# Sixteen tables of a graph layer, made four tiles earlier from the second group on

## The chip, the cores and the metric

One core of a Trainium2 chip. The metric is the device time in microseconds of one execution; lower is better. A profiled execution of the same kernel gives the durations below.

## The reference

Eight graphs share one adjacency matrix of 2048 nodes, with about nine neighbours for a node. Two attention layers follow each other, each with a residual and a layer norm. Layer 0 is scaled dot-product attention whose softmax runs apart in chunks of 256 nodes; layer 1 is a graph attention layer with leaky ReLU logits.

```python
# layer 0: x is (8, 2048, 256), 4 heads of 64, 8 chunks of 256 nodes
scores = clip(einsum('bhnd,bhjcd->bhnjc', q, kc) / 8, -10, 10)
scores = where(mask == 0, -10, scores)
attn = softmax(scores, axis=-1)                     # over each chunk
ctx = einsum('bhnjc,bhjcd->bhnd', attn, vc)
out = layernorm(ctx @ Wo.T + bo + x) * gamma + beta
x = layernorm(x + out)
# layer 1
e = leaky_relu(s_src[:, :, None, :] + s_dst[:, None, :, :], 0.2)
alpha = softmax(where(adj != 0, e, -inf), axis=2)
x = layernorm(x + elu(einsum('bijh,bjhd->bihd', alpha, Wh)))
```

## The kernel before

The adjacency is sparse, so the kernel builds lists of neighbours and gathers rows, in place of dense products. `edge_lists` runs first. It reads the 16 row tiles of the matrix, takes the largest 24 column numbers of each row on DVE, and ranks the nodes by their number of neighbours; each node's record is then scattered to HBM at its rank (L118, 16 indirect DMAs of POOL) and read back sorted (`srt`, L122). From `srt` come `node`, `idx`, `valid` and `same`. Sorted in this way, tile t of 128 nodes needs `CAPS[t]` neighbours, 24 for the first and 5 for the last.

The eight graphs are worked in four groups of two (`g` is 0 to 3), each with 16 tiles. For a group, **tables** have to stand in HBM: `tables(g, t)` makes keys and values (`kv_d[g]`, 512 KB a tile) and queries (`qx_d[g]`) of 128 rows. It loads `x` for two tiles at a time (L320), transposes it on PE (L336), copies it on ACT (L338, L341), multiplies on PE (L372, L376, L385, with biases by L313), copies to `kvs` (L367, L378, L379) and `qs` (L389) on ACT and stores both from SP's queue (L380, L391). `kvs` and `qs` have one buffer each, the PSUM tag `tk` has two. For every second tile POOL adds beta to `x` (L351) and SP stores the sum (L352). A table of group 1 holds a column more, the rank.

The tables of group 0 are made while the lists are: `edge_lists` calls `between(it)` after each of its 16 row tiles. The tables of group g+1 are made in the main loop, one with each tile of group g.

A tile of layer 0 goes through `fetch0` (POOL gathers one row of `kv_d` per neighbour, L489, and the queries, L527), `scores0` (products on DVE, L547 and L554, summed on PE, L566 and L576), `softmax0`, `context0` (weights on DVE, L501, or ACT, L507; sums on PE, L514; copy to `cT`, L626), and a tile later `finish0` and `rows1`, which writes the tables of layer 1. Gathered rows go into a ring of 14 units of two rows: 5 live in `ring0`, 9 in `ring1`, which takes the room that `edge_lists` has left and is zeroed first (L442 on ACT, L444 on DVE).

The main loop follows `seq`: 32 tiles of layer 0 (groups 0 and 1), then layer 0 of groups 2 and 3 with one tile of layer 1 between each two, then the rest of layer 1. `fetch(k + 1)` gathers for the next step ahead of this step's work. A gather may read any row of its table, so it waits for all 16 tiles of `kv_d[g]`. At the last tile of a group, `tables_first` holds the fetch back until the last table has been made. Instructions of one engine keep the order that a scheduler gives them, which follows the order of the program where the data allow no better.

The lines that carry this in the loop:

```python
tables_first = layer == 0 and seq[k + 1][0] == 0 and seq[k + 1][1] % NT == 0
if not tables_first:
    fetch(k + 1)
...
if g + 1 < NG:
    tables(g + 1, i % NT)
if tables_first:
    fetch(k + 1)
```

Of the kernel before, what the change touches and what calls it, by code (L numbers as in the profile page):

```python
# [9 lines left out]
F32 = mybir.dt.float32  # L10
# [7 lines left out]
P = 128  # L18
# [24 lines left out]

def edge_lists(tc: tile.TileContext, pool, bank, adj, const, ident, rec_d, B, between):

# [3 lines left out]
    NT = N // P  # L53
# [43 lines left out]
        between(it)  # L97


    rank = const.tile([P, NT], F32, name="rank")  # L100
    rank_i = pool.tile([P, NT], I32, name="rank_i")

    half = NT // 2
# [4 lines left out]
    for it in range(half):  # L108
        gt = pool.tile([P, N], F32, tag="v", name="v", bufs=2)
        nc.vector.tensor_scalar(gt, krow, key[:, it:it + 1], 0.0, op0=ALU.is_gt, op1=ALU.add,  # L110
                                accum_out=rank[:, it:it + 1])
        junk = pool.tile([P, N], BF16, tag="junk", name="junk", bufs=1)
        k = half + it
        nc.scalar.activation(junk, krow, AF.Sign, bias=nkey[:, k:k + 1], accum_out=rank[:, k:k + 1])
        nc.vector.tensor_scalar(rank[:, k:k + 1], rank[:, k:k + 1], 0.5, 0.5 * (N - 1), op0=ALU.mult, op1=ALU.add)
        nc.vector.tensor_copy(rank_i.rearrange("p (h t) -> p t h", h=2)[:, it], rank.rearrange("p (h t) -> p t h", h=2)[:, it])
        for k in (it, half + it):
            nc.gpsimd.indirect_dma_start(out=views[k],  # L118
                                         out_offset=bass.IndirectOffsetOnAxis(ap=rank_i[:, k:k + 1], axis=0),
                                         in_=rec[:, k, :], in_offset=None)  # L120
    srt = pool.tile([P, NT, REC], F32, name="srt")
    nc.sync.dma_start(srt, rec_d.rearrange("(t p) r -> p t r", p=P))  # L122

    vals = srt[:, :, 0:TOP]
    node = const.tile([P, NT], I32, name="node")
    nc.vector.tensor_copy(node, srt[:, :, TOP + 2])
    valid = const.tile([P, NT, TOP], I8, name="valid")
# [4 lines left out]
    idx = const.tile([P, NT, TOP], I32, name="idx")  # L132
    nc.vector.tensor_copy(idx, far)
    nodeb = const.tile([P, NT, 2 * G], I32, name="nodeb")
# [10 lines left out]
    same = []  # L145
# [21 lines left out]
    nc.tensor.matmul(op, nbad, ones, start=True, stop=True)  # L167
    over = const.tile([1, 1], I32, name="over")
    nc.vector.tensor_copy(over, op)
    return idx, valid, same, node, nodeb, rank, over  # L170


@with_exitstack
def sparse_path(ctx: ExitStack, tc: tile.TileContext, keep, x, adj, Wq, bq, Wk, bk, Wv, bv, Wo, bo, gamma, beta, W, a,
                out):
    nc = tc.nc
    B, N, F = x.shape
    KC = F // P
    NT = N // P
    NCH = N // CH  # L180
    NG = B // G
# [4 lines left out]
    rec_d = nc.dram_tensor("rec_d", [N, REC], F32).ap()  # L186
# [12 lines left out]
    const = ctx.enter_context(tc.tile_pool(name="const", bufs=1))  # L199
    ident = const.tile([P, P], F32, name="ident")  # L200
# [216 lines left out]
        tables(0, t)  # L417


    rings, turn = [ctx.enter_context(tc.tile_pool(name="ring0", bufs=1))], [0]  # L420

    def unit():
# [8 lines left out]

    with tc.tile_pool(name="lists", bufs=1) as pool:
        with nc.allow_low_precision("exact small integers"):
            idx, valid, same, node, nodeb, rank, over = edge_lists(tc, pool, bank, adj, const, ident, rec_d, B,
                                                             first_tables)
        nc.vector.tensor_copy(keep, over)

    rings.append(ctx.enter_context(tc.tile_pool(name="ring1", bufs=1)))
# [85 lines left out]
    def fetch0(g, t):  # L524
        units = gather(kv_d[g].shape[1], kv_d[g], idx, t)
        qx = work.tile([P, 2 * GF], F32, tag="qx", name="qx", bufs=4)
        nc.gpsimd.indirect_dma_start(out=qx, out_offset=None, in_=qx_d[g],  # L527
                                     in_offset=bass.IndirectOffsetOnAxis(ap=node[:, t:t + 1], axis=0))
        got0[g, t] = qx, units
# [80 lines left out]
    def context0(g, t):  # L610
        S = CAPS[t]
        al = st0.pop((g, t))
        units = got0[g, t][1]
        acc = bank("acc").rearrange("p (c r) -> p c r", r=P)

        na = len(units) // 4
        if g == PG:
            places(t, units)
        for u, s0, n in units[len(units) - na:]:
            weighted_act(u[:, :, GF:2 * GF], al, s0, n)  # L620
        for i, (u, s0, n) in enumerate(units):
            if i < len(units) - na:
                weighted(u[:, :, GF:2 * GF], al, s0, n)
            summed(acc, u[:, :, GF:2 * GF], s0 == 0, s0 + n == S)
        cT = work.tile([P, G * KC, P], F32, tag="cT", name="cT", bufs=1)
        nc.scalar.copy(cT, acc)  # L626
        st0[g, t] = cT
# [44 lines left out]
    def fetch1(p, t):  # L672
        got1[p, t] = gather(2 * WW, wh_d[p], idx1, t)

    def softmax1(p, t):
        S = CAPS[t]
        units = got1[p, t]
        z = small.tile([P, 2, GH, S], F32, tag="z1", name="z1")
        for u, s0, n in units:
            nc.vector.tensor_tensor(z[:, :, :, s0:s0 + n].rearrange("p k e s -> p s k e"),  # L680
                                    u.rearrange("p s (k w) -> p s k w", k=2)[:, :, :, GF:GF + GH],
                                    sd[p % 2][:, t].unsqueeze(1).to_broadcast([P, n, 2, GH]), op=ALU.add)
        z = z.rearrange("p k e s -> p (k e) s")
        nc.vector.scalar_tensor_tensor(z, z, SLOPE, z, op0=ALU.mult, op1=ALU.max)

        neg = small.tile([P, S], F32, tag="neg", name="neg")
        nc.vector.tensor_scalar(neg, valid[:, t, 0:S], -1.0, 1e30, op0=ALU.add, op1=ALU.mult)
        nc.vector.tensor_tensor(z, z, neg.unsqueeze(1).to_broadcast([P, 2 * GH, S]), op=ALU.add)
        m = small.tile([P, 2 * GH], F32, tag="m", name="m")
        nc.vector.tensor_reduce(m, z, axis=AX.X, op=ALU.max)  # L690
        nc.vector.tensor_tensor(z, z, m.unsqueeze(2).to_broadcast([P, 2 * GH, S]), op=ALU.subtract)
        e = z
        nc.scalar.activation(e, z, AF.Exp)
        nc.vector.tensor_tensor(e, e, valid[:, t, 0:S].unsqueeze(1).to_broadcast([P, 2 * GH, S]), op=ALU.mult)
        r = small.tile([P, 2 * GH], F32, tag="r", name="r")
        nc.vector.tensor_reduce(r, e, axis=AX.X, op=ALU.add)

        nc.vector.tensor_scalar(r, r, 1e-30, None, op0=ALU.max)
        nc.vector.reciprocal(r, r)
        nc.vector.tensor_tensor(e, e, r.unsqueeze(2).to_broadcast([P, 2 * GH, S]), op=ALU.mult)  # L700
        st1[p, t] = e
# [62 lines left out]
    seq = [(0, i) for i in range(2 * NT)]  # L764
# [24 lines left out]
    def scatters():  # L789
        for f in late:  # L790
            f()
        late.clear()

    def at(i):
        return i // NT, order[i % NT]

    def at1(i):
        return i // NT, order[i % NT] if i >= NT else order1[i]
# [3 lines left out]
    def fetch(k):  # L802

        while fetched[0] <= min(k, len(seq) - 1):
            layer, i = seq[fetched[0]]
            (fetch1(*at1(i)) if layer else fetch0(*at(i)))
            fetched[0] += 1
# [3 lines left out]
    for k, (layer, i) in enumerate(seq):  # L811
        g, t = at1(i) if layer else at(i)
        between = layer == 0 and seq[k + 1][0] == 1
        tables_first = layer == 0 and seq[k + 1][0] == 0 and seq[k + 1][1] % NT == 0
        if not tables_first:
            fetch(k + 1)
        scatters()
        if layer == 0:
            scores0(g, t)
            if between and i + 1 < NG * NT:  # L820
                softmax1(*at1(seq[k + 1][1]))
            if waiting is not None:

                if waiting:
                    finish1(*at1(waiting - 1))
                context1(*at1(waiting))
                waiting = None
            if i > 1:
                rows1(*at(i - 2))
            if i:  # L830
                finish0(*at(i - 1))
            if g + 1 < NG:
                tables(g + 1, i % NT)
            if tables_first:
                fetch(k + 1)
            softmax0(g, t)
            context0(g, t)
        elif seq[k - 1][0] == 0 and seq[k - 1][1] + 1 < NG * NT:
            waiting = i
        else:  # L840

            last = seq[k - 1] == (0, NG * NT - 1)
            if last:
                rows1(*at(NG * NT - 2))
                finish0(*at(NG * NT - 1))
            softmax1(g, t)
            if last:
                rows1(*at(NG * NT - 1))
            finish1(*at1(i - 1))
            context1(g, t)  # L850
            if i >= NT + 2:
                release(g - 1, i - NT - 2)
# [434 lines left out]
```

## Time and profile before

| what | us |
|---|---|
| median of 3 runs | 2400.64 |
| the three runs | 2385.87 to 2404.24 |
| profiled execution | 2397.55 |
| its span, first to last instruction | 2395.8 |
| `srt` issued, first gather of group 0 | 188.3, 195.2 |
| first `cT`, last `cT` of group 0 | 246.8, 617.5 |
| last `cT` of group 1, of group 2, of group 3 | 1002.1, 1448.1, 1951.6 |

The page of the profile gives busy time by engine over the span, a timeline in 40 slices, and groups of instructions by line. From the same trace come answers for a window: the busy time of each engine in it (the number of instructions in brackets), who waited for whom, and the instructions of an engine in order of time, each with its start, its duration and, in square brackets, the idle time ahead of it and what ended it. A busy PE counts matmuls with modelled ends, so it is not PE at its peak. `POOL` indirect DMAs are counted by the time of making their descriptors.

Two groups of the page around the tables:

```profile
L351 POOL TENSOR_TENSOR xt<-xt,beta_r 128x1024 f32<-128x1024 f32 x32 | 77.1, 2410 | 143.1 <-PE tk L336 126.3
L385 PE MATMUL tk<-wq,xT 128*128 128x256 f32 x512 | 145.2, 397 | 24.4 <-ACT kvs L379 24.4
```

Behind the shape stand the number of instructions, their busy time and mean duration in ns, the idle time ahead of them, and what ended most of it.

### The profile page before, as it was taken

The page shows a single profiled execution, that of the slowest core. Times are in us where ns is not written, and L with a number is a line of the kernel's source. Part 1 is how long each engine was busy: PE and PEld are TensorE (multiplying, and loading weights), DVE is VectorE, ACT ScalarE, POOL GpSimd, SP SyncE. Part 2 cuts the span into 40 slices and gives each one's busy share as a digit, 9 for nine tenths or more (in the row PEclk, how much of TensorE's full clock was granted, in tenths as well). Part 3 has the DMA queues.
Part 4 walks back from the last instruction along what each step waited for, and adds up shares of the span by engine and source line. Part 5 has one row for each costly group of instructions (what it writes and reads, how often), then busy time and mean ns, then how long its engine had stood idle before and what let it go on. Part 6 is the DMA issues. An engine that isn't in the chain of part 4 may idle for free. (4 is left out here: it accounts for less than half of the span.)

```text
span 2395.8 us, 38844 instructions
## 1 busy us (share of the span) xinstructions
PE 1900.4 (79%) x11946; PEld 1622.0 (68%) x11946; DVE 1833.5 (77%) x4099; ACT 1409.0 (59%) x5036; POOL 1505.0 (63%) x1230
## 2 busy tenths in 40 slices
PE   7686889889899898999988885888678786664764
PEld 5565677778778787777876774776566675554653
DVE  6864587877588988588988886887788887775775
ACT  4573455546566555655565665664356677665766
POOL 3125455672666676376668856774677685787883
PEclk9897899899999999999998997987878987877887
DMA  7737877795889798598879977896679896786884
GB/s 259 242 137 272 265 270 281 260 346 209 316 287 320 260 334 319 212 388 298 302 258 353 360 281 238 285 321 221 230 274 326 306 319 248 278 310 231 302 296 154
DMA packets 239982, 669.10 MB, mean 279 GB/s; under 512 B 43688, under 2 KB 70059, under 8 KB 237719
## 3 DMA queue, kind: packets, MB, share of 16 engines
q0 software_dynamic: 156800, 505.01, 60.1%
q1 hardware_dynamic: 79248, 151.55, 17.2%
q10 hardware_dynamic: 3718, 9.97, 1.3%
q8 instruction: 98, 1.61, 0.3%
q14 instruction: 118, 0.96, 0.1%
HBM read 612.79 MB, written 126.36 MB: 309 GB/s over the span
## 5 line engine op out<-in xcount | busy, mean ns | idle before, releaser
L489 POOL DMA_INDIRECT u<-kv_d,idx x656 | 810.2, 1235 | 436.4 <-PE acc L514 185.7
L514 PE MATMUL acc<-ident,u 128*128 128x128 f32 x5248 | 713.4, 291 | 157.0 <-DVE u L501 89.0
L514 PEld LDWEIGHTS acc<-ident,u 128*128 128x128 f32 x5248 | 637.5, 151 | 220.7 <-DVE u L501 133.2
L489 POOL DMA_INDIRECT u<-wh_d,idx x328 | 416.5, 1270 | 148.2 <-issue 76.4
L566 PE MATMUL pr<-ident,u 128*128 128x128 f32 (+1 forms) x1984 | 287.0, 295 | 78.7 <-DVE u L547 77.2
L501 DVE TENSOR_TENSOR u<-u,al 128x1024 f32<-128x1024 f32 x280 | 334.5, 1234 | 1.5
L566 PEld LDWEIGHTS pr<-ident,u 128*128 128x128 f32 (+1 forms) x1984 | 245.4, 151 | 110.8 <-DVE u L547 104.6
L547 DVE TENSOR_TENSOR u<-u,qx 128x1024 f32<-128x1024 f32 (+1 forms) x248 | 302.0, 1218 | 18.3 <-DMA u<-kv_d,idx 15.1
L501 DVE TENSOR_TENSOR u<-u,z 128x1024 f32<-128x1024 f32 x266 | 314.4, 1212 | 0.6
L507 ACT ACTIVATE u<-u,z 128x64 f32<-128x64 f32 x1008 | 262.0, 337 | 25.0 <-DVE z L700 17.1
L507 ACT ACTIVATE u<-u,al 128x64 f32<-128x64 f32 x800 | 209.1, 342 | 23.2 <-DVE al L607 22.3
L663 PE MATMUL mf<-wa,x1T 128*128 128x264 f32 x512 | 167.6, 455 | 23.1 <-ACT x1T L658 14.8
L351 POOL TENSOR_TENSOR xt<-xt,beta_r 128x1024 f32<-128x1024 f32 x32 | 77.1, 2410 | 143.1 <-PE tk L336 126.3
L385 PE MATMUL tk<-wq,xT 128*128 128x256 f32 x512 | 145.2, 397 | 24.4 <-ACT kvs L379 24.4
L451 ACT ACTIVATE nm<-sums 128x2 f32<-128x2 f32 (+1 forms) x160 | 32.4, 202 | 221.3 <-DVE sums L641 122.6
L372 PE MATMUL tk<-wkv,xT 128*128 128x256 f32 x512 | 151.7, 410 | 12.9 <-ACT xC L341 12.6
L635 PE MATMUL mf<-wo,cT 128*128 128x256 f32 x512 | 148.4, 415 | 6.3 <-ACT whs L666 5.3
L376 PE MATMUL tk<-wkv,xC 128*128 128x256 f32 x512 | 144.5, 399 | 0.0
L663 PEld LDWEIGHTS mf<-wa,x1T 128*128 128x128 f32 x512 | 101.7, 218 | 59.7 <-ACT x1T L658 23.6
L455 ACT ACTIVATE sq<-o,nm 128x256 bf16<-128x256 f32 x256 | 129.7, 507 | 5.3
L554 DVE TENSOR_TENSOR u<-u,qx 128x1024 f32<-128x1024 f32 (+1 forms) x96 | 116.0, 1214 | 16.6 <-DMA qx<-qx_d,node 7.1
L590 DVE TENSOR_SCALAR sc<-tf 128x64 f32<-128x64 f32 (+5 forms) x64 | 14.0, 218 | 138.2 <-PE tf L576 138.2
(168 smaller groups left out, 3254.0 us busy)
## 6 DMA issues: line engine op xcount, KB each, us to landing
kv_d<-kvs SPq DMA_DIRECT2D x48, 512.0 KB, 6.0
wh_d<-whs SPq DMA_DIRECT2D x64, 260.0 KB, 5.8
xt<-in_x_dram SPq DMA_DIRECT2D x64, 256.0 KB, 4.8
qx_d<-xt SPq DMA_DIRECT2D x32, 512.0 KB, 4.4
qx_d<-qs SPq DMA_DIRECT2D x64, 256.0 KB, 5.8
x_d<-o SPq DMA_DIRECT2D x64, 256.0 KB, 5.2
xr<-x_d SPq DMA_DIRECT2D x32, 512.0 KB, 4.9
u<-kv_d,idx POOLq DMA_INDIRECT x656, 6.5
```

Of the source, the lines that this page charges most:

```text
L372: nc.tensor.matmul(pm[:, 0:F], xT[:, b * KC + kc, rows], wkv[:, kc, 0:F], start=(kc == 0), stop=False, skip_group_check=True)
L376: nc.tensor.matmul(pm[:, F:], xC[:, b * KC + kc, rows], wkv[:, kc, F:], start=False, stop=(kc == KC - 1), skip_group_check=True)
L385: nc.tensor.matmul(qb, xT[:, b * KC + kc, rows], wq[:, kc, :], start=(b == 0 and kc == 0), stop=False, skip_group_check=True)
L455: nc.scalar.activation(sq, src[:, k, :], AF.Square, bias=nm[:, k:k + 1], accum_out=m2[:, k:k + 1])
L489: nc.gpsimd.indirect_dma_start(out=u[:, k, 0:width], out_offset=None, in_=table, in_offset=bass.IndirectOffsetOnAxis(ap=idx[:, t, s0 + k:s ...
L501: nc.vector.tensor_tensor(pv, pv, av, op=ALU.mult)
L507: nc.scalar.activation(pe, pe, AF.Copy, scale=al[:, e, s0 + k:s0 + k + 1])
L514: nc.tensor.matmul(acc[:, c, :], part[:, k, c * P:(c + 1) * P], ident, is_transpose=True, start=first and k == 0 and c == 0, stop=last and ...
L547: nc.vector.tensor_tensor(prod.rearrange("p k j (s w) -> p k j s w", w=W8), u[:, :, 0:GF].rearrange("p s (k j w) -> p k j s w", k=UNIT, w=W8),
L566: nc.tensor.matmul(pr[0:n * W8, k, :], prod[:, j // (NJ // UNIT), j % (NJ // UNIT), :], ident, is_transpose=True, start=(j == 0), stop=(j ...
L635: nc.tensor.matmul(po[:, b, :], cT[:, b * KC + kc, :], wo[:, kc, :], start=(b == 0 and kc == 0), stop=False, skip_group_check=True)
L663: nc.tensor.matmul(pw[:, 0:F + 2 * H], xT[:, b * KC + kc, :], wa[:, kc, :], start=(kc == 0), stop=(kc == KC - 1))
```

## The change

`edge_lists` gets one more function to call, `behind`. It is called after the 16 scatters and ahead of the load of `srt`; it makes the tables (1,0) to (1,3). In the main loop, the tile with number i then makes the table that lies 4 further on than before: tables(g+1, t) with t from 4 to 15, and after them the first four of group g+2. Tiles 44 to 47 make none. The fetch of the next step stands ahead of the step's work in every case. `rank`, which the tables of group 1 read, is now allocated ahead of `edge_lists` and passed in.

```diff
-def edge_lists(tc, pool, bank, adj, const, ident, rec_d, B, between):
+def edge_lists(tc, pool, bank, adj, const, ident, rec_d, rank, B, between, behind):
...
-    rank = const.tile([P, NT], F32, name="rank")
     rank_i = pool.tile([P, NT], I32, name="rank_i")
...
                                          in_=rec[:, k, :], in_offset=None)
+    behind()
     srt = pool.tile([P, NT, REC], F32, name="srt")
     nc.sync.dma_start(srt, rec_d.rearrange("(t p) r -> p t r", p=P))
...
+    LEAD = 4
+
+    def lead_tables():
+        for t in range(LEAD):
+            tables(1, t)
+
+    rank = const.tile([P, NT], F32, name="rank")
...
-        tables_first = layer == 0 and seq[k + 1][0] == 0 and seq[k + 1][1] % NT == 0
-        if not tables_first:
-            fetch(k + 1)
+        fetch(k + 1)
...
-            if g + 1 < NG:
-                tables(g + 1, i % NT)
-            if tables_first:
-                fetch(k + 1)
+            if i + NT + LEAD < NG * NT:
+                tables(*divmod(i + NT + LEAD, NT))
             softmax0(g, t)
```

More of the change, by code (lines that the diff above doesn't have):

```diff
@@ L42, with edge_lists @@
 EMIN = 4.5399929762484854e-05
-def edge_lists(tc: tile.TileContext, pool, bank, adj, const, ident, rec_d, B, between):
+def edge_lists(tc: tile.TileContext, pool, bank, adj, const, ident, rec_d, rank, B, between, behind):
     nc = tc.nc
@@ L169, in edge_lists @@
     nc.vector.tensor_copy(over, op)
-    return idx, valid, same, node, nodeb, rank, over
+    return idx, valid, same, node, nodeb, over
 @with_exitstack
@@ L433, in sparse_path @@
         with nc.allow_low_precision("exact small integers"):
-            idx, valid, same, node, nodeb, rank, over = edge_lists(tc, pool, bank, adj, const, ident, rec_d, B,
-                                                             first_tables)
+            idx, valid, same, node, nodeb, over = edge_lists(tc, pool, bank, adj, const, ident, rec_d, rank, B,
+                                                             first_tables, lead_tables)
         nc.vector.tensor_copy(keep, over)
```

## The prediction, made before the result was known

> **What bounds the kernel now.** I read the totals of the page first, then the busy time in stretches cut at the milestones of the tiles, then the waits of the opening, and last the timelines of ACT and POOL at the two places that the change touches.
>
> ```profile
> PE 1900.4 (79%) x11946; PEld 1622.0 (68%) x11946; DVE 1833.5 (77%) x4099; ACT 1409.0 (59%) x5036; POOL 1505.0 (63%) x1230
> ```
>
> No engine is full over the whole span, so the stages have to be read apart. The columns below are PE, weight load, DVE, ACT and POOL busy, the granted clock, the share of the DMA engines and GB/s.
>
> ```profile
> 176.00:187.00 11.00, 0.21 (x1) 0.00 (x0) 0.00 (x0) 0.58 (x3) 8.23 (x8) 0.73 0.51 177
> 187.00:200.00 13.00, 11.61 (x47) 9.17 (x48) 3.34 (x16) 5.15 (x21) 3.86 (x4) 0.63 0.50 134
> ...
> 210.00:222.00 12.00, 4.16 (x13) 3.19 (x14) 9.64 (x8) 10.67 (x11) 6.30 (x6) 0.72 0.76 259
> ...
> 357.00:617.00 260.00, 232.59 (x1491) 200.10 (x1490) 199.04 (x375) 139.70 (x520) 145.58 (x115) 0.93 0.76 264
> 617.00:1002.00 385.00, 349.80 (x2249) 300.19 (x2248) 306.15 (x617) 227.61 (x896) 241.94 (x190) 0.96 0.83 296
> ...
> 1300.00:1399.00 99.00, 85.65 (x581) 74.73 (x582) 80.85 (x166) 63.52 (x234) 79.54 (x60) 0.93 0.95 352
> ...
> 1460.00:1490.00 30.00, 13.62 (x63) 11.42 (x64) 18.02 (x53) 16.78 (x60) 14.75 (x14) 0.61 0.60 206
> ```
>
> From 357 to 1002 us (groups 0 and 1) PE is busy 232.6 + 349.8 of 645 us, 90%: PE bounds there, and work that is moved from one of these tiles to another gains nothing. The opening has room: from 176 to 300 us PE is busy 89.3 of 124 us. The hole at 1460 to 1490 us comes just after the third group boundary.
>
> The waits of the opening (194 to 300 us: who waited for whom, total, times, longest):
>
> ```profile
> DVE sc L590 <- PE tf L576: 26.6, 4, 11.2
> ACT kvs L367 <- DMA kv_d<-kvs: 22.8, 4, 8.6
> POOL u L489 <- PE acc L514: 17.5, 3, 16.9
> PEld tf L576 <- ACT prT L572: 13.4, 4, 6.2
> ```
>
> These are one chain. ACT may refill kvs, which has one buffer, only when its table has landed; behind that wait on ACT stands the copy prT (L572), for it waits PE, for PE waits DVE. The boundary into group 3, on POOL's timeline:
>
> ```profile
> 1401.81 2.37 POOL L351 TENSOR_TENSOR xt<-xt,beta_r 128x1024 f32<-128x1024 f32 x1
> 1416.46 1.87 POOL L489 DMA_INDIRECT u<-wh_d,idx  x1 [12.27 <-ACT sq L455]
> ...
> 1432.85 1.00 POOL L489 DMA_INDIRECT u<-kv_d,idx  x1 [7.82 <-issue]
> ```
>
> POOL gathers almost nothing from 1400 to 1433 us, because the first tile of group 3 needs the whole of kv_d3, whose last piece is issued at 1425.7 us. The longest PE wait of 1399 to 1500 us, 14.0 us for the weighted u of L501, is the hole above. The same gap of POOL stands at the first boundary (557.0 to 610.1 us) and the second (940.3 to 994.0), but there PE goes on at 90%.
>
> **What the Trainium skill says.** "TensorE: Matmul & The Clock Gate", in its table ahead of the first section, gives ScalarE and GpSimd a strict first-in first-out queue: so one wait for kvs holds everything behind it. The trace agrees: the exp of the first tile comes after three such waits. The same page, "What's actually happening", says that idle time brings the clock down: here 0.61 in the hole at 1460 us against 0.96 in group 1. "SBUF — State Buffer", "The DMA setup-cost knee", fits a transfer as 2 us plus bytes over 436 GB/s: for a 512 KB table an estimate of 3.2 us. The trace has 6.2 us as median, under other traffic, and 7.5 to 8.6 us from issue to ACT's next copy in the opening. I use the trace.
>
> **The change, part by part.** I also read the order of the instructions of both compiled programs, engine by engine.
>
> *Price of a table, from its lines at full clock.* PE, from 154.7 to 160.7 us, takes 6.1 us for one, and 0.6 us of transposes: 6.7 us. ACT: 4 copies of 0.37, one of 0.59, 0.19 for the rank column, and half a pair of chunk_x, 2 x (0.39 + 0.2 + 0.49) = 2.2: 4.4 us. POOL: half of a 2.4 us beta addition. SP: two stores, half of two loads and of a store. DVE: none, apart from one small sum in the last tile of a group. Nothing is added or removed in all: 64 tables stay 64, and SP, ACT and POOL issue the same DMAs in another order.
>
> *Opening.* The old program already makes tables (1,0) and (1,1) here: their pieces go out at 203.9 and 221.8 us. So the change moves two more ahead of the first context, and the rest of the four by the sixth tile: counted on ACT at the first cT, 19 tables before and 21 after, at tile 5 22 and 26. Of PE, 4 x 6.7 = 27 us are put into a stretch with 34.7 us idle (124 - 89.3), but ACT's queue decides: ahead of the first exp stand 5 waits of L367 for kvs in place of 3, and ahead of the first cT 6 in place of 4. Followed along ACT: L367 of (1,1) at 211.3 as before; (1,2) at 221, as one turn of kvs takes 7.5 us to land and some 2 us of copies and issue; now the zeroing of ring1 on ACT (L442, 5 x 1.93 us), which started at 212, starts here, so POOL's gathers into ring1, that waited for it until 214.2, go on at 223; (1,3) at 234; (1,4) at 244, and then the exp, at 232.3 before: +12. The first cT comes at about 254.5, before at 246.8: +8. Two tables are still to be caught up until tile 5, 13 us of PE, of which the 12% idle of these 100 us may take most. POOL also has one beta addition (2.4 us) ahead of the first gather and one between the gathers of tiles 0 and 1, each waiting for PE; they end before L442 does. SP: the read of the flag and the stores of group 1 change places; the flag is read at the end only. I take **+11 us**; bounds +3 (PE catches up in idle time) and +27 (all four in series).
>
> *First two boundaries.* The fetch of the next tile now stands ahead, its table complete four tiles earlier. What the gap costs: tiles 20 to 27 of group 1 (105 records) took 212.9 us from cT to cT, tiles 28 to 31 (30 records) 84.1; so a tile costs 13.6 us and a record 0.99. Tiles 15 to 19 (35 records) ought to take 102.7 and took 105.9; tiles 31 to 35 took 102.9. The gap costs 3.2 + 0.2: **-3 us**; the 14 ring units cover the rest. Bounds 0 and -12 (PE's dip of about 5 us at 610 to 660 and 3 us at 1010, with the slow clock).
>
> *Third boundary.* Here layer 1 runs beside, and behind tile 48 stand 24 gathers of one layer-1 tile at 1.3 us each. Pairs of tiles in group 3 (no tables) took 6.3 us + 1.81 per record, fitted to tiles 51 to 62; pairs (47,48) and (49,50) with 22 and 39 records took 53.2 and 80.2, 7 and 3 over it: **-10 us**. Bounds -3 and -25, nearly the 30 us for which POOL stood.
>
> *Four tables fewer beside tiles 39 to 47* (ACT's counts: 8.5 before, 5 after). PE is 87% busy at 1300 to 1399, DVE 82%, POOL 80%: not one bound. By the fit, pairs (43,44) and (45,46) took 6.4 us too long each with some 1.5 tables, pairs (39,40) and (41,42) took 9 and 5 less than it. I take 2.3 us for each of 3.5 tables: **-8 us**; bounds 0 and -24 (3.5 x 6.7).
>
> Sum: 11 - 3 - 10 - 8 = **-10 us**. The profiled execution took 2397.55 us (span 2395.8 and 1.75 around it), which gives 2387.6; it lies 3.1 us under the median of the three runs, 2400.64, which gives 2390.6. I say 2389.
>
> **Rivals.** *Faster by over 1%*: the opening takes the tables in idle time (+3), and the boundaries and the emptier third stretch give most of their bounds (-8, -20, -18): -43, 2357 from the median. For it speak the 34.7 us of idle PE and the 33 us without gathers; against it PE's 90% and the covered first boundaries. *Slower*: ACT's queue with the single kvs buffer becomes the bound of the opening. If each of the four tables costs its whole turn of 9.5 us there, the tiles start 38 us late, and as PE bounds until 1002 us nothing is caught up; with 8 us of gain later this is +30, 2430. It is over 1% from a cost of 24 us above the later gains on. For it speaks the 22.8 us already spent in this wait and two more waits ahead of the first tiles; against it that PE, not ACT, is full from tile 5 on. *It does little*: the order found by the scheduler already filled the gap, so opening and ends cancel: 2398 to 2403.
>
> **How the numbers follow.** About 1% (24 us) is what a measurement of this kernel can tell from no change, as its three runs lie 18 us apart. Forecast with small gain 0.40 and little change 0.17: within 1% 0.57. Faster case 0.25, slower case 0.18. The range from 2352 to 2430 reaches the centres of both; the likeliest case alone spans 2375 to 2405.
>
> **What would show it.** The first exp at about 244 and first cT near 254 us; kv_d1 complete near 520 us and no gap of POOL above 15 us at the three boundaries; the hole after 1460 us gone; from the fourth group on the same distances from cT to cT as now. It would be wrong if the first tiles come over 25 us late, if tiles 5 to 15 still fall back, or if the hole only moves to another layer-1 tile.

## The result, and the profile after

The changed kernel takes 2404.07 us (median of 20 runs, 2391.76 to 2415.28). The kernel before, now with 20 runs of its own, takes 2386.57 (2377.1 to 2404.24), 14 us under the median of its first three. The ratio is 1.0073, 95% interval 1.0053 to 1.0092: a loss of 17.5 us, where a gain of 10 was summed. On some chips a part of the runs takes longer, so ratios compare only the runs within 1.5% of the fastest of the same kernel.

Lines up to some 340 of the changed kernel are the old number plus 1, those of the loop plus 11. First the totals of the page, then the waits of the opening (194 to 310 us; total, times, longest):

```profile
PE 1893.1 (79%) x11946; PEld 1629.1 (68%) x11946; DVE 1833.6 (76%) x4099; ACT 1410.2 (59%) x5036; POOL 1500.4 (62%) x1230
```

```profile
POOL u L500 <- PE acc L525: 25.5, 4, 9.7
ACT kvs L368 <- DMA kv_d<-kvs: 23.5, 7, 7.0
```

The busy times are those of before within 0.5%, so the loss lies in waits. ACT's wait for `kvs` comes 7 times, not 4, and takes as long. The milestones say where time went; all are starts of copies to `cT`, one profiled execution for each column. after_again and a_pl2 are two runs told of below:

| stretch, by tiles | before | after | after_again | a_pl2 (copies pinned) |
|---|---|---|---|---|
| first `cT` | 246.8 | 253.5 | 254.9 | 252.8 |
| to the end of group 0 (tile 15) | 617.5 | 617.4 | 616.9 | 617.0 |
| group 1 (15 to 31) | 384.6 | 395.9 | 393.3 | 381.4 |
| of it first boundary, 15 to 17 | 51.4 | 41.0 | 42.7 | 42.0 |
| of it 17 to 23 | 134.6 | 159.1 | 155.6 | 141.9 |
| group 2 (31 to 47) | 446.0 | 448.7 | 449.9 | 447.1 |
| of it second boundary, 31 to 33 | 47.0 | 40.3 | 41.6 | 42.3 |
| of it 33 to 41 | 223.0 | 242.9 | 242.3 | 238.6 |
| of it 41 to 47 | 176.0 | 165.5 | 166.0 | 166.2 |
| group 3 (47 to 63) | 503.5 | 494.1 | 489.8 | 493.6 |
| of it third boundary, 47 to 49 | 83.5 | 79.3 | 79.4 | 80.7 |
| span | 2395.8 | 2403.4 | 2396.5 | 2385.7 |

The change does what it says: the boundaries are shorter, and the opening costs nothing by tile 15. But in group 1 the 10 us won at its start are more than lost six tiles later. Busy times in a stretch of that group (PE, weight load, DVE, ACT, POOL, clock, share of the DMA engines, GB/s), before and then after:

```profile
620.00:800.00 180.00, 166.03 (x1050) 142.36 (x1051) 145.57 (x303) 109.33 (x435) 118.86 (x98) 0.95 0.93 333
```

```profile
620.00:800.00 180.00, 154.11 (x942) 132.20 (x941) 133.98 (x280) 97.11 (x384) 90.08 (x74) 0.93 0.75 265
```

Every engine does less, and the DMA engines too: 108 matmuls fewer in the same 180 us. No resource is full, so something stands in a queue. The instructions that wait tell which. `places` copies the rank column out of each gathered unit (`pl`) on ACT, for group 1 alone. What ACT stood idle for ahead of these copies (us, times), before and after:

```profile
L479 ACT COPY pl<-u x86: 175/193/277, 617.4 to 960.3; 128x2 f32<-128x2 f32 x78, 128x1 f32<-128x1 f32 x8
...
  DVE idx L481: 11.8, 5
  DMA u<-kv_d,idx: 10.5, 9
```

```profile
L490 ACT COPY pl<-u x86: 175/193/261, 572.5 to 971.5; 128x2 f32<-128x2 f32 x78, 128x1 f32<-128x1 f32 x8
...
  DMA u<-kv_d,idx: 53.1, 20
```

The same 86 copies of 0.19 us; but the first comes at 572.5, right behind the `cT` of tile 13 and long before the end of group 0, and ACT waits 53.1 us for gathers to land, five times as long. The timeline shows what stands behind one such wait, with PE's next product between the lines of ACT (start, duration, instruction, idle time ahead of it):

```profile
696.52 1.09 ACT L481 ACTIVATE o<-o,nm,r 128x256 f32<-128x256 f32 x2 [3.30 <-DVE nm L479]
704.36 0.19 ACT L490 COPY pl<-u 128x2 f32<-128x2 f32 x1 [6.75 <-DMA u<-kv_d,idx]
704.46 0.58 ACT L669 COPY x1T<-tf 128x512 f32<-128x512 f32 x1
...
705.09 2.13 PE L674 MATMUL mf<-wa,x1T 128*128 128x264 f32 x4 [4.06 <-ACT x1T L669]
...
707.25 0.37 ACT L675 COPY whs<-mf 128x256 f32<-128x256 f32 x1 [2.13 <-PE mf L674]
```

`x1T` (L669) goes out straight behind the copy; PE's next product (L674) needs it, and `whs` needs that. PE had finished what `x1T` copies at 700.4. So ACT's 6.75 us of waiting for data of a coming tile held the tile that was being finished, and cost PE 4.06 us. In the order of ACT's compiled instructions the 86 copies stand this many contexts (copies to `cT`) ahead of their own: 10 none, 68 one, 8 two before; 6 none, 35 one, 29 two, 16 three after. My reading is that with the tables complete earlier the scheduler took the gathers, and so the copies, to be ready earlier, and put them where it saw room on ACT; the order is read off, its reason is not shown.

### The profile page after: what moved, and what is told of

It reads as the page before. It is cut to its first block, busy times and chain, and to the rows that moved or that the text cites. A ratio compares the mean times of both kernels' runs of the same rounds, so it can differ in the third digit from the quotient of the medians.

```text
span 2403.4 us, 38836 instructions
## 1 busy us (share of the span) xinstructions
PE 1893.1 (79%) x11946; PEld 1629.1 (68%) x11946; DVE 1833.6 (76%) x4099; ACT 1410.2 (59%) x5036; POOL 1500.4 (62%) x1230
## 3 DMA queue, kind: packets, MB, share of 16 engines
q1 hardware_dynamic: 79248, 151.55, 17.2%
## 5 line engine op out<-in xcount | busy, mean ns | idle before, releaser
L500 POOL DMA_INDIRECT u<-kv_d,idx x656 | 798.2, 1217 | 410.8 <-PE acc L525 226.2
L558 DVE TENSOR_TENSOR u<-u,qx 128x1024 f32<-128x1024 f32 (+1 forms) x248 | 294.7, 1188 | 54.2 <-DMA u<-kv_d,idx 52.7
L512 DVE TENSOR_TENSOR u<-u,al 128x1024 f32<-128x1024 f32 x280 | 334.2, 1226 | 1.1
L512 DVE TENSOR_TENSOR u<-u,z 128x1024 f32<-128x1024 f32 x266 | 314.5, 1212 | 0.5
L577 PEld LDWEIGHTS pr<-ident,u 128*128 128x128 f32 (+1 forms) x1984 | 251.8, 153 | 85.9 <-DVE u L558 78.5
L518 ACT ACTIVATE u<-u,z 128x64 f32<-128x64 f32 x1008 | 262.0, 337 | 30.3 <-DVE z L711 29.2
L674 PE MATMUL mf<-wa,x1T 128*128 128x264 f32 x512 | 164.4, 447 | 29.2 <-ACT x1T L669 15.8
L538 POOL DMA_INDIRECT qx<-qx_d,node x64 | 75.1, 1173 | 123.3 <-DVE o L658 51.8
L674 PEld LDWEIGHTS mf<-wa,x1T 128*128 128x128 f32 x512 | 99.2, 213 | 66.7 <-ACT whs L677 26.8
L565 DVE TENSOR_TENSOR u<-u,qx 128x1024 f32<-128x1024 f32 (+1 forms) x96 | 113.4, 1184 | 34.0 <-DMA qx<-qx_d,node 17.2
```

What stands on the lines that cost most here:

```text
L500: nc.gpsimd.indirect_dma_start(out=u[:, k, 0:width], out_offset=None, in_=table, in_offset=bass.IndirectOffsetOnAxis(ap=idx[:, t, s0 + k:s ...
L512: nc.vector.tensor_tensor(pv, pv, av, op=ALU.mult)
L518: nc.scalar.activation(pe, pe, AF.Copy, scale=al[:, e, s0 + k:s0 + k + 1])
L558: nc.vector.tensor_tensor(prod.rearrange("p k j (s w) -> p k j s w", w=W8), u[:, :, 0:GF].rearrange("p s (k j w) -> p k j s w", k=UNIT, w=W8),
L577: nc.tensor.matmul(pr[0:n * W8, k, :], prod[:, j // (NJ // UNIT), j % (NJ // UNIT), :], ident, is_transpose=True, start=(j == 0), stop=(j ...
L674: nc.tensor.matmul(pw[:, 0:F + 2 * H], xT[:, b * KC + kc, :], wa[:, kc, :], start=(kc == 0), stop=(kc == KC - 1))
```

## The experiments

Ratios are to the kernel before on the same chip. The chips differ: the kernel before takes 2589 us on the first of these five, 2382 on the second, 2593, 2528 and 2580 on the later ones. Only ratios of one chip are set beside each other. ("Call" in an expectation stands for the runs on one chip.) "Pinned" means one edit, which makes the scheduler keep the copy where the program has it on ACT:

```diff
-            nc.scalar.copy(pl[:, s0:s0 + n], u[:, :, 2 * GF])
+            tc.keep_in_program_order(nc.scalar.copy(pl[:, s0:s0 + n], u[:, :, 2 * GF]))
```

**First chip: the copies, or the query gathers.** a_pl pins the copies in the changed kernel, b_pl in the kernel before. a_qx pins, in the changed kernel, the gather of the queries behind the row gathers of its tile, since POOL's idle time ahead of it had grown from 64 to 123 us; a_plqx pins both.

```diff
-        nc.gpsimd.indirect_dma_start(out=qx, out_offset=None, in_=qx_d[g],
-                                     in_offset=bass.IndirectOffsetOnAxis(ap=node[:, t:t + 1], axis=0))
+        tc.keep_in_program_order(
+            nc.gpsimd.indirect_dma_start(out=qx, out_offset=None, in_=qx_d[g],
+                                         in_offset=bass.IndirectOffsetOnAxis(ap=node[:, t:t + 1], axis=0)))
```

> The changed kernel, with the copies of the gathered ranks (the pl copies of group 1) held in program order on ACT, behind the exp of their own tile. Theory A (these copies stand up to three tiles too early on ACT, which waits 53 us in 20 times for gathers to land, and that is where the loss of group 1 comes from): the waits of these copies for gathers fall from 53 us to under 10 us, group 1 (last cT of group 0 to last cT of group 1) falls from 396 us to 385 us or less, and the whole by 10 to 20 us, to a ratio of 0.995 to 1.002 against the kernel before. Theory B (the query gathers stand too early in POOL's queue): under 4 us of change. Theory C (the opening costs the loss): under 4 us of change, ratio about 1.007.

> The kernel before with the same copies held in program order: the control. There only 8 of 86 copies stand two contexts ahead and their waits for gathers were 10.5 us. Theory A: little to gain, within 5 us of the kernel before (ratio 0.998 to 1.002). Theories B and C: the same; if it gains 10 us or more, holding the copies is good in itself and says nothing of the change.

> The changed kernel, with each query gather (qx, four buffers) held in POOL's queue behind the row gathers of its own tile. POOL stood 122 us ahead of these gathers, in the kernel before 64. Theory B: this idle time falls to about 60 us, row gathers start earlier, and the whole gains 8 to 18 us (ratio about 1.000). Theory A: under 4 us, as ACT still waits for the same gathers. Theory C: under 4 us.

> The changed kernel with both held. If A and B are each part of the loss the gains add: 15 to 25 us, ratio 0.993 to 1.000, faster than the kernel before, and the distances from cT to cT in groups 1 and 2 no longer than before. If A alone holds: the same as with the copies alone, within 4 us. Theory C: still 1.005 to 1.009.

Measured: a_pl 0.9846 (0.9778 to 0.9914), b_pl 1.0008 (0.9978 to 1.0037), a_qx 1.0428 (1.0375 to 1.0481), a_plqx 1.0381 (1.0330 to 1.0433). a_pl gains more than any case foresaw (its ratio rests on 3 of 6 runs; by the medians of all runs it is 0.987), and a_qx and a_plqx went against all of them. The query gathers that stand early are no loss in this form: holding them back costs 4%. The copies look like the cause, but the changed kernel itself was not run on this chip.

**Second chip: with and without the pin, and the opening.** after_again is the changed kernel, a_pl2 the pinned one. late_pl is pinned and makes the four leading tables after the lists instead of ahead of the sorted read; lead1_pl is pinned and leads by one table (`LEAD = 1`).

```diff
-                                                             first_tables, lead_tables)
+                                                             first_tables, lambda: None)
...
+    lead_tables()
```

> The changed kernel again, beside its pinned form on one chip, profiled there. Theory A (rank copies pl sent ahead on ACT cost the loss): 1.005 to 1.015 of the kernel before, and at least 1.2% behind the form with pinned copies in the same call; ACT waits over 45 us for gathered u ahead of the pl copies, over 100 us of POOL idle ahead of the query gathers of group 1. Theory C (the opening costs the loss): as slow as the pinned form within 0.5%. If the pin gained only because that chip differs, this run comes near 0.985 too.

> The changed kernel with the rank copies kept in program order on ACT, once more. Theory A: 0.978 to 0.992 of the kernel before as in the first call, and 1.2 to 3% under the changed kernel beside it; ACT waits under 15 us ahead of the pl copies; cT from tile 15 to 31 no longer than before's 385 us on this chip plus 3. Theory C: no better than the changed kernel, since the opening is the same in both.

> Rank copies pinned, and the four leading tables made after the lists are done, ahead of the first tile, in place of ahead of the sorted read. Theory A says the opening is worth little in all: within 0.5% (12 us) of the pinned form. Theory C: the place in the opening decides, so this differs from the pinned form by more than 12 us; faster if the two further tables stood in the way of the first gathers, slower (by up to 38 us, four turns of kvs) if the wait for the sorted records hid them.

> Rank copies pinned, lead of one table in place of four: the opening is nearly that of the kernel before, the next table still stands before the boundary fetch. If the boundaries carry the gain (prediction: 13 us for three), this is 0.990 to 0.997 of the kernel before, and the pinned form with lead 4 lies within 0.5% of it. If the emptier last tiles of the third group carry it (8 us for four tables fewer), lead 1 keeps a quarter of that and lies 6 us or more behind lead 4.

Measured: after_again 2399.33 us, 1.0073 (1.0050 to 1.0097); a_pl2 2387.14 us, 1.0011 (0.9987 to 1.0034). The pin gives back 12.2 of the 17 us. That is half a per cent, less than half of the 1.2% foreseen for this pair, though within the 10 to 20 us foreseen for a_pl. In a_pl2 no copy waits any more:

```profile
L490 ACT COPY pl<-u x86: 175/189/275, 623.0 to 981.3; 128x2 f32<-128x2 f32 x78, 128x1 f32<-128x1 f32 x8
...
its engine sat idle before it (us, times) until:
who waited for it (us, times):
```

The list of idle times is empty, and group 1 takes 381.4 us, 11.9 less than in after_again, which is the whole gain; groups 0, 2 and 3 differ by under 4 us. The stretch from 620 to 800 us again:

```profile
620.00:800.00 180.00, 163.27 (x1050) 142.01 (x1050) 143.46 (x303) 106.99 (x424) 100.52 (x78) 0.96 0.81 286
```

1050 matmuls, as before the change. POOL's idle time ahead of the query gathers, which I had taken to be a consequence of the copies, is not: it is 116.2 us here and 122.5 in after_again. What goes with the copies is POOL's wait for PE ahead of row gathers, from 617 to 1085 us 71.9 in after_again and 30.3 in a_pl2.

late_pl takes 2407.73 us, 1.0100 (1.0074 to 1.0127), 20.6 us behind a_pl2. 13.6 of them are there at tile 15 (630.6 us against 617.0), and group 1 takes 7.2 us longer. So the place in the opening is worth something, as theory C had it: made while the records are on their way, four tables cost nothing by tile 15; made right ahead of the loop, they do. lead1_pl takes 2417.76, 1.0149 (1.0111 to 1.0188), 30.6 us behind a_pl2. That is the case "6 us or more" by its number, but only in part for its reason. At tile 12 it falls 15 us back, and the timelines of PE and SP show why:

```profile
536.32 1.04 PE L577 MATMUL pr<-ident,u 128*128 128x128 f32 x8
...
542.18 0.90 SPq L321 DMA_DIRECT2D xt<-in_x_dram  x2
...
549.93 0.69 PE L337 MATMUL tk<-ident,xt 128*128 128x128 f32 x2 [12.58 <-DMA xt<-in_x_dram]
```

A transpose for a table, placed before the load of `x` has landed (issued only at 542.18), holds PE and the products of the current tile behind it for 12.6 us. It is the same fault on another engine. Group 1 takes 12.8 us longer than in a_pl2, with no copy waiting, and for that no run shows a cause; group 2 takes 9.3 us longer, beside whose last tiles lead1_pl has three tables more to make, and group 3 takes 5.0 less.

**Third chip: a second profile of before, and the last tables.** before_again is the kernel before, b_pl2 its pinned form, and tail1_pl the pinned form with lead 4 in groups 1 and 2 and lead 1 in group 3:

```diff
-            if i + NT + LEAD < NG * NT:
+            if i < 2 * NT - LEAD:
                 tables(*divmod(i + NT + LEAD, NT))
+            elif 2 * NT - 1 <= i < 3 * NT - 1:
+                tables(NG - 1, i - 2 * NT + 1)
```

> The kernel before once more, for a second profile: the profiled execution shown lies 11 us over the median of its 20 runs. Theory A expects the extra time to lie in some few steps of group 2 or later, and the distances of groups 0 and 1 (617.5 and 384.6 us) to come again within 4 us, so that the loss of the changed kernel in group 1 (11 us) stands. If group 1 alone varies by 10 us between executions, the loss can't be placed by these milestones.

> The kernel before with the rank copies kept in program order, as control to the pinned changed kernel on the same chip. Theory A: there the copies stand at most two contexts ahead, so the pin is worth nothing: 0.997 to 1.003. Rival (the pin is a gain of its own, whatever the tables): 0.993 to 0.996, which would leave the change itself a loss of 0.5% also with pinned copies.

> Rank copies pinned, lead of four tables in groups 1 and 2 and of one in group 3, so that the tiles 44 to 46 make a table each as in the kernel before and the opening is that of the changed kernel. Prediction's term for four tables fewer beside tiles 39 to 47: 8 us, and 10 us for the third boundary, which is kept here by one table's lead. If the 8 us are real, this is 6 to 8 us slower than the pinned form with lead 4 (1.0011 of the kernel before), so 1.003 to 1.005; if the tables gain nothing where they are left out, it is within 2 us of it.

The chip was one of the slower kind (before 2593 us), so the first of these did not answer: its stretches are all longer. b_pl2 came at 0.9897 (0.9849 to 0.9945) and tail1_pl at 0.9775 (0.9711 to 0.9839). That b_pl2 gains 1% here is against the expectation of a neutral control. But this ratio rests on 6 of its 22 runs; by the medians of all runs it is 0.997, so a gain of the pin on the kernel before is not shown.

**Fourth chip: all four forms side by side** (before 2528 us).

> Rank copies pinned, lead 4 in groups 1 and 2, lead 1 in group 3, now beside the form with lead 4 throughout. On a chip whose kernel before takes 2385 us: if four tables fewer beside tiles 44 to 47 are worth the 16 us that the traces suggest, this is 0.5 to 0.7% slower than lead 4 throughout; if the query gathers that stand early in POOL's queue in group 2 (31 us of POOL's waits with lead 4, 10 us before) are the other side of it, this loses nothing and is equal or up to 0.7% faster. On a chip whose kernel before takes 2590 us: 0.97 to 0.985 again, and the same two cases.

> Pinned form with lead 4 throughout, as reference for the other three of this call: 0.9987 to 1.0034 of the kernel before on a chip where that takes 2385 us, 0.978 to 0.991 where it takes 2590 us.

> The changed kernel on the same chip. Theory A: 0.4 to 0.9% behind its pinned form on either chip. On a chip where the kernel before takes 2590 us[...], the copies wait longer, so the distance grows to over 1%. If the pin is worth nothing there, the changed kernel stands at 0.985 too.

> Control: the kernel before with pinned copies, on the same chip as its pinned counterpart. Within 0.4% of the kernel before where that takes 2385 us (the copies stand at most two contexts ahead there); 0.985 to 1.004 where it takes 2590 us, as in the two calls so far.

Measured: after_3 2512.00 us, 0.9964 (0.9933 to 0.9996); a_pl3 2485.32, 0.9860 (0.9809 to 0.9911); b_pl3 2524.84, 0.9978 (0.9951 to 1.0005); tail1_pl2 2495.37, 0.9882 (0.9827 to 0.9937). The pin takes 26.7 us off the changed kernel and 3.2 off the kernel before, so here too it mends what the change brought. Where, the traces do not tell: the profiled executions of after_3 and a_pl3 have spans of 2510.1 and 2511.0 us, as that of a_pl3 lies 27 us over its median, and ACT stands idle for 49 us ahead of the copies of after_3, less than the 57 on the first profile after. And on this chip the change itself gains, a little: its sign seems to depend on the chip. One part of it is seen in the traces: from tile 15 to 17 b_pl3 (the kernel before, pinned) takes 71.1 us and after_3 42.3, so the first boundary gains 29 us here in place of 10, of which 8.6 are left at the end of group 1. Why it gains more, and why such a chip is slower at all, no run shows.

tail1_pl2 and a_pl3 are not told apart by their intervals. Their traces show two opposite terms: from tile 33 to 41 tail1_pl2 takes 239.0 us and a_pl3 260.2, from 41 to 47 186.4 and 174.3. That looks as if beginning group 3's tables three tiles later spared the first stretch 21 us and cost the second 12. But it is one execution each, that of a_pl3 a slow one by 27 us; and lead1_pl, which makes group 3's tables beside the same tiles as tail1_pl2, takes 242.7 us from tile 33 to 41 on the second chip, no less than a_pl2 there. So this cause of the first term is not shown.

**Fifth chip** (before 2580 us): a third profile of before, the control, and a pinned lead of two tables (`LEAD = 2`).

> The kernel before once more, for a profile nearer its median. If the chip is one where it takes 2385 us, some step between the tiles 16 and 63 takes up to 11 us less than in the profile shown, and so tells which term of the sum (opening, boundaries, tables left out) the pinned form really lost. On another chip it only gives a second pair of traces.

> Control on the kernel before, once more. So far 1.0008, 0.9897 and 0.9978 on chips where the kernel before takes 2589, 2593 and 2528 us. On a chip where it takes 2385 us: 0.997 to 1.003.

> Rank copies pinned, lead of two tables. On a chip where the kernel before takes 2385 us lead 1 stood at 1.0149 and lead 4 at 1.0011. If the loss of lead 1 comes from one load of x that PE waits for at tile 11 (15 us) and from the tables left beside the last tiles, lead 2 lies between, 1.003 to 1.010. If a smaller opening is worth something by itself, it lies at 0.998 or under.

Measured: b_pl4 1.0009 (0.9968 to 1.0050); lead2_pl 0.9929 (0.9901 to 0.9958). The control is neutral on three chips of four by its ratio, and on all four by the medians of all runs (0.996 to 0.999). Lead 2 gains here too, but the chip isn't the one of lead 1 and 4, so the question of the opening stays with late_pl. before_3 is again a profile of a slower chip.

## Why the prediction was wrong

**The step that failed** is the line that nothing is added or removed and the same DMAs are only issued in another order, and with it the term of the first two boundaries that rests on it, "The gap costs 3.2 + 0.2: -3 us; the 14 ring units cover the rest. Bounds 0 and -12". I priced the moved instructions, and took all others on their queues as standing where they stood. But a table that is complete earlier makes everything behind it early as well: the gathers and, in group 1 alone, the rank copies on ACT. Their new place cost 12.2 us on the second chip (the pin gave back 26.7 on the fourth), and the bounds of this term allowed no loss at all. I had read the order of both compiled programs, but looked there for tables and DMAs, not for instructions that the diff doesn't name.

That is not all of it. With the copies pinned the change is worth between 3 us less and 8 us more (0.9987 to 1.0034), still not -10. A second step is missing from the sum: it has no term for the tiles 33 to 41, and they take 15.6 us longer with the pin and 19.9 without (below).

**The base.** The sum started from a profiled execution of 2397.55 us, which lies 11.0 us over the later median of 2386.57. This shifts the predicted time, not the predicted change. By the table above a_pl2's span is 10.1 us under that execution's, while by medians the two kernels are level: so some of what the table shows as gains, probably in group 3 where no tables are made (tiles 49 to 63 take 420.0 us before and 412.9 in a_pl2), is this execution's own. That is argued; no second profile of before on such a chip shows it.

**Term by term**, with that in mind:

- *Opening, +11 us.* At the first exp, foreseen at 244, it came at 242.0, and the first `cT`, foreseen at 254.5, at 253.5. The delay was right (+6.7 at the first `cT`), but not that it stays: by tile 8 it is gone. That "PE, not ACT, is full from tile 5 on" took a mean of 90% for a full engine; from 420 to 530 us PE was busy 90.6 of 110 us before, and 97.7 after. The term should have been 0.
- *First two boundaries, -3 us.* They gained 10.4 and 6.7 us by their own stretches; POOL's gap is gone, the first gathers of group 1 start at 559.3 in place of 610.1. But those stretches are too short to count by. With the copies pinned the first boundary gains 9.4 us, of which the tiles 17 to 23 give back 7.3, and group 1 as a whole gains 3.2: the size that was set down. (The second gains 4.7, and the tiles 33 to 41 lose 15.6 behind it.) What the term lacked is the copies, for which the tiles 17 to 23 take another 17.2 us (159.1 against 141.9).
- *Third boundary, -10 us.* It gained 4.2. The 30 us for which POOL gathered almost nothing are filled, as POOL's timeline of the changed kernel shows:

```profile
1406.57 1.01 POOL L500 DMA_INDIRECT u<-kv_d,idx  x1 [3.52 <-PE acc L525]
...
1431.81 1.96 POOL L500 DMA_INDIRECT u<-wh_d,idx  x1 [0.30 <-DVE r L471]
...
1470.98 1.00 POOL L500 DMA_INDIRECT u<-wh_d,idx  x1 [0.30 <-issue]
...
1473.63 1.02 POOL L500 DMA_INDIRECT u<-kv_d,idx  x1 [0.31 <-PE acc L525]
```

  but the hole after it is there still, and was never the boundary's. The waits from 1410 to 1512 us:

```profile
PE acc L525 <- DVE u L512: 26.6, 7, 15.1
```

  The layer-1 tile gathers its 24 records from 1431.8 to 1472 us; its softmax runs over all of them, so DVE can weight the first (L512) only at 1495.24, and PE waits 15.1 us, 14.0 before. Tile 49's row gathers, issued behind the layer-1 tile's, start at 1473.6, at 1469.9 before. The stall's releaser was in the profile of before; the term took what lay next to it in time for its cause.
- *Four tables fewer beside tiles 39 to 47, -8 us.* Tiles 41 to 47 gained 10.5 us, in which as many fewer tables are made. Right in kind and nearly in size. But tiles 33 to 41 lost 19.9, in a_pl2 too (15.6), and this no step foresaw; by their stores nine tables are made beside them in place of eight, which at 6.7 us of PE for one explains a third at most. The windows of 33 to 41, before and after:

```profile
1049.00:1272.00 223.00, 202.60 (x1378) 174.90 (x1379) 193.13 (x373) 133.24 (x496) 151.01 (x118) 0.98 0.86 305
```

```profile
1052.00:1296.00 244.00, 218.24 (x1403) 192.04 (x1402) 187.95 (x376) 140.79 (x522) 148.09 (x119) 0.92 0.79 279
```

  PE runs 25 matmuls more, 2%, and is busy some 15 us longer, with a granted clock of 0.92 in place of 0.98. The page "TensorE: Matmul & The Clock Gate" of the Trainium skill, "What's actually happening", puts a lower clock down to idle time. The mean busy share hardly differs (91% and 89%), but single stalls do, and the trace agrees with the page. PE's waits in the two windows for `prT`, before and after, and one piece of the window after in which the clock is down:

```profile
PE tf L576 <- ACT prT L572: 0.2, 1, 0.2
```

```profile
PE tf L587 <- ACT prT L583: 10.3, 4, 4.2
1151.60:1158.40 6.80, 5.72 (x19) 4.99 (x20) 5.31 (x13) 5.14 (x21) 3.38 (x4) 0.50 1.03 399
```

  After, the clock is at one half in six such pieces, 37.5 us in all (from 1100.4, 1151.6, 1178.9, 1216.5, 1250.6 and 1260.8 us); before, in two, 6.8 us. Each begins during a stall of PE or within 2 us of its end. At half clock 30.7 us more cost PE an estimated 15 us, which is what it was busy longer. So the loss is that of short stalls, 4 us at the longest, multiplied by the clock. Why `prT` comes later on ACT there, and in the pinned forms too, no run shows.

**The rivals.** "Slower" named a loss on the same engine and for the same reason, one wait in ACT's first-in first-out queue with work of the current tile behind it, but at the opening and for `kvs`. That wait grew by 0.7 us. That the predicted time, 2389, lies only 15 us under the measured one is luck: its base was 11 to 14 us too high, and the change itself was missed by 27.5 us.

**What the changed kernel lacks** is the pin. With it, it is level with the kernel before on the chip where that takes 2382 us (1.0011), and beats it by 1.4 to 1.5% on two of the slower ones, as it beats the changed kernel on both chips on which they were run together, by 0.5 and 1.1%. Without the changed order of the copies the change is thus worth nothing on one chip and a per cent or so on others.

## What to carry to other kernels

If a change makes some data ready earlier, list everything that a scheduler may then move, consumers on other engines above all, and look in the compiled order for instructions placed ahead of a DMA that the trace shows to land late: on an in-order queue each of them holds the work of now for data of later. A copy of 0.19 us is no small thing there; what counts is the wait ahead of it, and pinning it cost nothing measurable in the kernel before, where most copies stood one tile ahead. And a gap of one engine beside a stall of another is no cause until the stalled instruction's own releaser has been followed back. Nor does a gain in the stretch where a change acts count as a gain before the stretches behind it have been added.

## What the runs showed of the hardware

One program takes from 2382 to 2593 us (medians) on five chips, and a change of schedule seems to have another sign on them: the changed kernel 1.0073 (1.0050 to 1.0097) on one and 0.9964 (0.9933 to 0.9996) on another. The mean granted clock of before was 0.885 in its first profile and 0.858 and 0.859 in the two of slower chips. Of the 202 us by which the span of before_again is longer, PE's busy time has 54 (1954.3 us in place of 1900.4), DVE's and ACT's 4 and 5; so most of it is waiting, and for what, these traces leave open. A few per cent learned on one chip are shown for that chip alone.

In two of these traces a stall of PE of some 3 us costs more than itself. From tile 8 to the last `cT`, every one of 3 us or more (16 in the profile of before, 22 in that of after) overlaps a piece at half clock or is followed by one within 3.5 us; of the shorter ones, from 1 us on, 29 of 46 and 28 of 46.
